# Attention, cumulative-max attention and expert choice on one core: where two candidate lists are merged, and how the last sample is searched

## The chip, the cores and the metric

The kernel runs on one core of a Trainium2 chip. The metric is the device time of one execution in microseconds; lower is better. A core has five engines that run their own instruction streams: PE (TensorE, matmuls and transposes), DVE (VectorE), ACT (ScalarE), POOL (GpSimd) and SP (SyncE, which here only issues DMAs). Streams are tied together by semaphores.

## The reference

The input is four samples of 128 channels by 64x64 positions, so 4 x 4096 tokens of 128 numbers. Three steps follow one another, each with a residual:

```python
x = x + conv_attn(group_norm(x))      # three 1x1 convs, 4096x4096 softmax attention
t = tokens(x)
t = t + cummax_attn(layer_norm(t))    # 8 heads: exp(s - cummax(s)), cumsum, v weighted, mean of heads
t = t + expert_choice(layer_norm(t))
```

The change lies in the last step. It is an expert choice: the experts choose the tokens.

```python
logits = einsum('bsd,ed->bse', x, gate_w) + gate_b      # 64 experts
probs = softmax(logits, axis=1)                          # over the 4096 tokens of a sample
vals, idx = top_k(probs.transpose(0, 2, 1), 8)           # 8 tokens for each expert
pooled = einsum('bked,bke->bed', x[idx], vals)           # weighted sum of those 8 tokens
h = gelu([pooled, 1] @ weight1[e])                       # 129 x 512, own weights for each expert
out = [h, 1] @ weight2[e]                                # 513 x 128
outputs.at[idx].add(out * vals)                          # scattered back to the 8 tokens
```

For every sample and expert the kernel needs the eight largest logits, their rows, the sum of the exponentials of all 4096 logits, and the eight rows of x weighted and summed. The weights of the 64 experts are 512 KB each.

## The kernel before, in words

The first layer takes the span to about 1450 us and is not touched. Then `loop` (L2150) goes over 32 blocks of 512 tokens: four samples of eight blocks. It is software-pipelined: in one turn PE does the keys (`f_pk`) of the block six ahead, and for the block itself the values (`f_pv`, 64 matmuls in each of four parts), the totals (`f_pt`), the products (`f_po` L1174, L1186), and the carried sums (`f_ltr`, `f_str`, `f_etr`, `f_mc`). The turn ends when DVE adds the result into `t` (L1192). The order on every engine is the order of the program: PE, ACT, DVE and POOL are written out by hand, as is the order of DMAs on SP.

The gate (norm, logits, choice) runs beside this, some blocks behind. `make_plan` (L2091) puts each of its steps into a slot of a block: `at(i, slot, fn, ...)` notes it, and `run(m, slot)` emits it. The slots of a turn are 1, 2, "D", 3, 4, "T" and "G" in that order. The steps of the gate are:

- `gate_stats`, `gate_root`, `gate_close`: mean and root of the variance of each token.
- `gate_norm` (ACT L1272, or DVE L1267): the normalised rows `f_x`, stored by SP to a table in DRAM, `f_table`.
- `gate_turn` (L1281): four transposes `f_gtr` and a copy to SBUF (L1285).
- `gate_logits` (L1287): `f_pl`, then DVE writes the logits `f_lg` (L1295) and takes the eight largest of this block (MAX8, L1299). A partition holds one expert; the two halves of 64 partitions hold two halves of a block's tokens.
- `merge_half` (L1311): the eight largest over the blocks of a sample, for each half. `candidate_rows` (L1326): `max_index` over all logits of the sample (2048 a partition, `f_ci`).
- `merge_halves` (L1336): `both_halves` brings the two halves together with eight small matmuls `f_pw` (L1320), then some fourteen small DVE operations make the final eight values and their row numbers `f_at`.
- `gathers` (L1370): four indirect DMAs on POOL fetch rows from the table. `exps` (L1377): exponentials of all logits. `count`, `denominators`, `select` (L1397), `pool` (L1440, `f_pp`): weights and the pooled rows.

All of `f_pl`, `f_pw`, `f_mc`, `f_etr`, `f_pq`, `f_pp` and `f_htr` share one PSUM buffer with the tag "sm".

The last sample can't wait for a later block. Its first seven blocks are merged in slot "T" of block 31, and `last_choice` (L1474) does the rest after the loop: the norm and logits of block 31, a merge of its eight best with those found before, the exponentials, and pooling (`f_pp`, `f_ce`, `f_pc`). Between these stand `fill`s (L1460): transposes `f_etb` of `t` that are wanted later, put back by `put_back` (L1465). Then `experts` (L1625) takes 16 groups of four experts: `f_ph`, gelu, `turn` (`f_htr`), `f_eo`, and one or two `turn_back`s (`f_otr`). `late_choice` (L1556) does what is left of the last sample's counting on DVE beside the first groups. Twenty-one experts have rooms that can be filled from block 26 on (`load_into`, `load_rooms` L2224); the other 43 are loaded in halves when `f_ph` and `f_eo` have freed a room (L1597, L1604). `stores` writes the output.

Of the kernel before, what the change touches and what calls it, by code (L numbers as in the profile page):

```python
# [17 lines left out]
def conv_attn_hybrid_kernel(  # L18
# [809 lines left out]
    def fast():  # L828
# [365 lines left out]
        def gate_setup(rest):  # L1194
# [28 lines left out]
            for j in range(16):  # L1223
                nc.gpsimd.memset(spare(3, 48 + j, 1), float(j))
# [35 lines left out]
        def gate_norm(m, split=False):  # L1260
            b, k = blocks[m]
            x2_of[m] = x2 = env.xl_pool(f"f_x2_{m}")
            for c in range(CPB):
                src = t[:, b * NCH + k * CPB + c, :]
                rs, nb = env.grs[:, ring(m), c : c + 1], env.gnb[:, ring(m), c : c + 1]
                if split and c % 2:
                    nc.vector.tensor_scalar(  # L1267
                        out=x2[:, c, :], in0=src, scalar1=rs, scalar2=nb,
                        op0=ALU.mult, op1=ALU.add,
                    )  # L1270
                else:
                    nc.scalar.activation(x2[:, c, :], src, AF.Identity, bias=nb, scale=rs)  # L1272
            if not split:
                rows_ = table[b].rearrange("(h k c p) d -> h k p c d", h=2, k=deep[b], p=P)
                for h in range(2):
                    nc.sync.dma_start(out=rows_[h, k], in_=x2[:, 2 * h : 2 * h + 2, :])
# [10 lines left out]
        def gate_logits(m):  # L1287
# [11 lines left out]
            nc.vector.max(out=sel[b]["cand"][:, bass.ts(k, 8)], in_=env.lg[b][:, k, :])  # L1299

        ex_at = lambda i: env.e2b[:, bass.ts(i, BLK)]
        g_at = lambda k: env.e1b[:, 5 * BLK + k * C : 5 * BLK + (k + 1) * C]
# [8 lines left out]
        def merge_half(b, count):  # L1311
            st = sel[b]
            st["both"] = both = small_tile(b, "both", 16, bufs=1)
            nc.vector.max(out=both[:, 0:8], in_=st["cand"][:, : count * 8])
# [11 lines left out]
        def candidate_rows(b, count):  # L1326
            st = sel[b]
            both = st["both"]
            ci = small_tile(b, "ci", 8, dtype=U32, bufs=1)
            nc.vector.max_index(out=ci, in_max=both[:, 0:8], in_values=flat_lg(b, 0, count))  # L1330
            nc.vector.tensor_scalar(
                out=both[:, 8:16], in0=ci, scalar1=env.base[:, b : b + 1], scalar2=None,
                op0=ALU.add,
            )

        def merge_halves(b):  # L1336
            st = sel[b]
            pw = both_halves(st["both"], f"f_pw_{b}").rearrange("p s (v k) -> p v s k", v=2)
            found = spare(3, 0, 32).rearrange("p (v s k) -> p v s k", v=2, s=2)
            nc.vector.tensor_copy(found, pw)  # L1340
            first8 = spare(3, 32, 16).rearrange("p (v k) -> p v k", v=2)
            st["top"] = top = first8[:, 0]
            vals, rows16 = spare(3, 0, 16), spare(3, 16, 16)
# [7 lines left out]
            for h in range(2):  # L1351
                half = slice(h * E, (h + 1) * E)
                nc.vector.tensor_copy(own[half], first8[half, :, 4 * h : 4 * h + 4])
            st["src"] = src = small_tile(b, "src", 5, bufs=1)
            nc.vector.tensor_copy(src[:, 0:4], own[:, 0])
            nc.vector.tensor_copy(src[:, 4:5], top[:, 7:8])
            hit = spare(2, 0, 64).rearrange("p (k j) -> p k j", k=4)
            nc.vector.tensor_tensor(
                hit, own[:, 1].unsqueeze(2).to_broadcast([P, 4, 16]),
                spare(3, 48, 16).unsqueeze(1).to_broadcast([P, 4, 16]), ALU.is_equal,  # L1360
            )
            nc.vector.tensor_tensor(
                hit, hit, rows16.unsqueeze(1).to_broadcast([P, 4, 16]), ALU.mult,
            )
            rowf = small_tile(b, "rowf", 4, bufs=1)
            nc.vector.tensor_reduce(rowf, hit, AX.X, ALU.add)
            st["at"] = at = small_tile(b, "at", 4, dtype=I32, bufs=1)
            nc.vector.tensor_copy(at, rowf)

        def gathers(b, lo, hi):  # L1370
            for k in range(lo, hi):
                nc.gpsimd.indirect_dma_start(
                    out=g_at(k), out_offset=None, in_=table[b],
# [3 lines left out]
        def exps(b, j):  # L1377
            st = sel[b]
            if j == 0:
                st["ce"] = ce = small_tile(b, "ce", 5, bufs=1)  # L1380
                st["sums"] = small_tile(b, "sums", 4, bufs=1)
                nc.scalar.activation(ce, st["src"], AF.Exp, bias=st["neg"])
# [57 lines left out]
        def pool(b):  # L1440
            dd = sel[b]["dd"]
            pp = sm(f"f_pp_{b}", E)
            for k in range(4):
                nc.tensor.matmul(pp, g_at(k), dd[:, k, :], start=(k == 0), stop=(k == 3))
# [28 lines left out]

        def last_choice():  # L1474
# [5 lines left out]
            for n, tag in enumerate(("kv", "kv", "kv", "kv", "t", "o", "kv", "kv")):  # L1480
                fill(n, tag, n % 2)
            put_back(0, act, 2)
            gate_root(m, 1)
            gate_close(m, 1)
            gate_norm(m, split=True)
            put_back(2, act, 2)
            gate_turn(m, dve)
            fill(8, "kv")
            gate_logits(m)
            put_back(6, act, 2)  # L1490
            fill(9, "kv", 1)
            late = st["cand"][:, bass.ts(k, 8)]
            pw = both_halves(late, "f_pw1")
            fill(10, "kv")
            fill(11, "kv", 1)
            merged = small_tile(b, "merged", 24, bufs=1)
            nc.vector.tensor_copy(merged[:, 0:8], top0)
            nc.vector.tensor_copy(merged[:, 8:24], pw.rearrange("p s k -> p (s k)"))
# [7 lines left out]
            st["ce"] = ce = small_tile(b, "ce", 5, bufs=1)  # L1506
            nc.scalar.activation(ce, src, AF.Exp, bias=neg)
            nc.scalar.activation(chd, lg, AF.Exp, bias=neg)
            st["sums"] = sums = small_tile(b, "sums", 4, bufs=1)
            nc.scalar.activation(  # L1510
                flat_lg(b, 0, NBLK), flat_lg(b, 0, NBLK), AF.Exp, bias=neg,
                accum_out=sums[:, 0:1],
            )
            put_back(4, act)
            put_back(10, act, 2)
# [4 lines left out]
                out=chd, in0=chd, scalar=ce[:, 4:5], in1=chd, op0=ALU.is_ge, op1=ALU.mult  # L1520
            )
            pp = sm("f_pp3", E)
            for kk in range(4):
                nc.tensor.matmul(pp, g_at(kk), dd[:, kk, :], start=(kk == 0), stop=False)
            pc = ps.tile([P, BLK], F32, tag="x", name="f_pc")
            for j in range(2):
                nc.tensor.transpose(pc[:, bass.ts(j, P)], chd[:, bass.ts(j, P)], ident)
            ct = ex_at(1)[:, HB:].rearrange("p (j x) -> p j x", j=2)
            nc.vector.tensor_copy(ct, pc[:, : 2 * P].rearrange("p (j x) -> p j x", j=2))
            x2 = x2_of[NB - 1]  # L1530
            for h in range(2):
# [5 lines left out]
                if h == 0:  # L1537
                    pq = ps.tile([P, BLK], F32, tag="x", name="f_pq3")
                    nc.tensor.matmul(pq[:, 0:1], env.pair, sums[:, 0:1], start=True, stop=True)
            nc.vector.reciprocal(env.den[:, b : b + 1], pq[:, 0:1])  # L1540
            dr = env.e1b[:, 7 * BLK + 2 * C : 7 * BLK + 2 * C + E]
            nc.vector.tensor_scalar(
                out=dr, in0=env.pair[:, :E], scalar1=env.den[:, b : b + 1], scalar2=0.5,
                op0=ALU.mult, op1=ALU.mult,
            )
            pr = ps.tile([P, BLK], F32, tag="t", name="f_pr3")
            nc.tensor.matmul(
                pr[:, :E], ones.to_broadcast([P, P]), dr, start=True, stop=True
            )
# [6 lines left out]
        def late_choice(g):  # L1556
            if g < 2:
                count(B - 1, g, g + 1)
            elif g == 2:
                select(B - 1)  # L1560

        def late_count():
            b = B - 1
            pq = sm("f_pqb", 2)
            nc.tensor.matmul(pq, env.pair, sel[b]["sums"][:, 2:4], start=True, stop=True)
# [59 lines left out]
        def experts():  # L1625
# [9 lines left out]
            hold = [  # L1635
                env.rest.tile([P, FC, QG, QW], F32, tag="xl", name=f"f_hs_{i}", bufs=3)
                for i in range(2)
            ]
            for tile_ in hold:
                nc.gpsimd.memset(tile_, 0.0)  # L1640
# [79 lines left out]
            n = 12  # L1720
            for g in range(EG):
                turn(g)
                late_choice(g)
                for _ in range(2 if g < NB - 12 - EG else 1):
# [366 lines left out]
        def make_plan():  # L2091
# [14 lines left out]
            at(NB - 1, 1, gate_root, NB - 2, 1)  # L2106
            at(NB - 1, 1, gate_close, NB - 2, 1)
# [4 lines left out]
            for m in range(NB - 10, NB - 2):  # L2112
                i = NB - 5 + (m - NB + 10) // 2
                at(i, "D" if m == NB - 6 else "G", gate_norm, m)
                at(i + 1, 1 + m % 2, gate_turn, m)
                at(i + 1, (2 if i == NB - 2 else 3) + m % 2, gate_logits, m)
            at(NB - 1, 2, gate_norm, NB - 2)
            at(NB - 1, 3, gate_turn, NB - 2)
            at(NB - 1, 4, gate_logits, NB - 2)
            for b in range(B - 2):  # L2120
# [3 lines left out]
                at(i, 3, merge_halves, b)  # L2124
                at(i, 4, exps, b, 0)
                for k in range(4):
                    at(i + k, "G", gathers, b, k, k + 1)
# [13 lines left out]
            at(NB - 2, "G", select, last)  # L2141
            at(NB - 1, 1, denominators, last)
            at(NB - 1, 4, pool, last)
            at(NB - 1, 4, merge_half, B - 1, NBLK - 1)
            at(NB - 1, 4, candidate_rows, B - 1, NBLK - 1)
            at(NB - 1, "T", merge_halves, B - 1)
            at(NB - 1, "T", gathers, B - 1, 0, 4)
            at(NB - 1, "T", root_table)

        def loop():  # L2150
            make_plan()
            normals(LAG + 1)
            for n in range(LAG, NB + LAG):
# [13 lines left out]
                value(m, 0)  # L2167
                value(m, 1)
                slot(2)
                if n < NB:  # L2170
# [27 lines left out]
                totals(2)  # L2198
                totals(3)
# [16 lines left out]
                if n == NB + 2:  # L2216
                    load_into(slot_of(env.e1a, 2))
                if n == NB + LAG - 2:
                    load_into(slot_of(env.e1a, 3))
# [4 lines left out]
        def load_rooms():  # L2224
            for room in (slot_of(env.ama, 0), slot_of(env.ama, 1), slot_of(env.ama, 2),
                         slot_of(env.ama, 3), env.wvs,
                         env.held[:, bass.ts(3, HD)]):
                load_into(room)
            for i in range(CPB):
                load_into(slot_of(env.amb, i))  # L2230
            load_into(slot_of(env.e2a, 0))
            load_into(slot_of(env.e2a, 1))
# [93 lines left out]
```

## Time and profile before

| what | value |
|---|---|
| time, median of 3 runs (lowest, highest) | 2317.12 us (2316.6, 2318.71) |
| profiled execution, its own time | 2323.74 us |
| its span, first to last instruction | 2322.0 us |
| mean granted TensorE clock | 0.992 |
| PE, DVE, ACT, POOL busy | 97%, 62%, 47%, 8% of the span |
| block, from one addition to `t` to the next | 20.9 to 22.4 us in most blocks |
| block 14 and block 22 | 27.4 and 29.8 us |
| first `f_ph` of the experts | 2222.69 us |
| last expert weight landed | 2289.9 us |

The page's durations are those of one execution, which took 6.6 us longer than the median of the runs. In a row of the timeline or of the costliest groups the letters after the line number say what was written from what ("f_pw<-f_both,ident"), and the bracket at the end gives the idle time of that engine just before, and what ended it. "PEclk" is the clock that was granted, as a share of the full one.

### The profile page before, as it was taken

The page shows a single profiled execution, that of the slowest core. Times are in us where ns is not written, and L with a number is a line of the kernel's source. Part 1 is how long each engine was busy: PE and PEld are TensorE (multiplying, and loading weights), DVE is VectorE, ACT ScalarE, POOL GpSimd, SP SyncE. Part 2 cuts the span into 40 slices and gives each one's busy share as a digit, 9 for nine tenths or more (in the row PEclk, how much of TensorE's full clock was granted, in tenths as well). Part 3 has the DMA queues.
Part 4 walks back from the last instruction along what each step waited for, and adds up shares of the span by engine and source line. Part 5 has one row for each costly group of instructions (what it writes and reads, how often), then busy time and mean ns, then how long its engine had stood idle before and what let it go on. Part 6 is the DMA issues. An engine that isn't in the chain of part 4 may idle for free.

```text
span 2322.0 us, 43150 instructions
## 1 busy us (share of the span) xinstructions
PE 2247.8 (97%) x18352; PEld 1168.5 (50%) x18352; DVE 1444.6 (62%) x2361; ACT 1086.4 (47%) x1324; POOL 175.9 (8%) x364
## 2 busy tenths in 40 slices
PE   7999999999999999999999999999999999999997
PEld 3544444444444444444444444456565556556663
DVE  7666565655665565565556656568777677865623
ACT  2343333433333443334455444455666566566641
POOL 0000000000000000000000000012211222122311
PEclk9999999999999999999999999999999999999989
DMA  2000010000010000000000000011122121114578
GB/s 77 32 12 17 9 45 8 17 8 9 17 45 9 9 17 9 9 25 27 9 5 5 10 5 5 20 44 41 41 58 53 43 59 46 52 47 129 153 279 303
DMA packets 78555, 104.77 MB, mean 45 GB/s; under 512 B 8976, under 2 KB 44816, under 8 KB 78352
## 3 DMA queue, kind: packets, MB, share of 16 engines
q1 hardware_dynamic: 77264, 99.81, 14.0%
q8 instruction: 146, 2.39, 0.4%
q0 software_dynamic: 512, 1.05, 0.2%
q10 hardware_dynamic: 576, 1.05, 0.1%
q14 instruction: 57, 0.47, 0.1%
HBM read 78.55 MB, written 17.04 MB: 41 GB/s over the span
## 4 chain that ended last, share of the span: by engine, by line
PE 86%; DVE 6%; ACT 3%; DMA 3%; issue 1%; SPq 0%; POOL 0%; another core or an unknown queue 0%; ACTq 0%; DVEq 0%; POOLq 0%
PE av L1939 36%; PE sc L1914 18%; PE f_pv L1128 9%; PE f_pk L973 8%; PE f_pt L1151 3%; PE f_po L1174 2%; PE pd L1965 1%; DMA x<-in_x_dram 1%; ACT f_e1a L980 1%; PE pa L1887 1%; PE pe L1861 1%; PE f_po L1186 1%; DVE f_e1a L981 1%; DVE f_e1a L982 1%; PE f_pl L1291 1%
## 5 line engine op out<-in xcount | busy, mean ns | idle before, releaser
L1939 PE MATMUL av<-pr,am 64*128 64x512 f32 x4096 | 978.0, 592 | 2.9 <-ACT pr L1919 2.9
L1919 ACT ACTIVATE pr<-sc 128x1024 f32<-128x1024 f32 x512 | 523.6, 1023 | 782.7 <-PE sc L1914 769.8
L1926 DVE TENSOR_TENSOR acc<-acc,pr 128x1024 f32<-128x1024 f32 x480 | 586.6, 1222 | 485.4 <-ACT pr L1919 481.1
L1939 PEld LDWEIGHTS av<-pr,am 64*128 64x128 f32 x4096 | 401.6, 187 | 472.9 <-issue 457.9
L1914 PE MATMUL sc<-e,e 64*128 64x512 f32 x2048 | 534.4, 591 | 4.7 <-DMA e<-side 4.7
L1914 PEld LDWEIGHTS sc<-e,e 64*128 64x128 f32 x2048 | 201.6, 187 | 236.6 <-issue 229.0
L1128 PE MATMUL f_pv<-f_held,f_ama 128*32 128x256 f32 x4096 | 242.7, 387 | 5.5 <-ACT f_e1a L980 4.5
L973 PE MATMUL f_pk<-f_held,f_ama 128*128 128x512 f32 x512 | 234.9, 603 | 0.0
L1133 ACT ACTIVATE f_amb<-f_pv 128x1024 f32<-128x1024 f32 x128 | 130.8, 1023 | 141.7 <-PE f_pv L1128 140.9
L981 DVE TENSOR_TENSOR f_e1a<-f_e1a,f_held 128x1024 f32<-128x1024 f32 x128 | 157.5, 1231 | 46.6 <-ACT f_e1a L980 46.2
L980 ACT ACTIVATE f_e1a<-f_pk 128x1024 f32<-128x1024 f32 x128 | 129.9, 1025 | 117.8 <-PE f_pk L973 57.8
L1128 PEld LDWEIGHTS f_pv<-f_held,f_ama 128*32 128x32 f32 x4096 | 131.3, 111 | 102.2 <-issue 15.1
L982 DVE TENSOR_REDUCE f_e1a<-f_e1a 128x8 f32<-128x1024 f32 x128 | 155.3, 1218 | 3.5
L973 PEld LDWEIGHTS f_pk<-f_held,f_ama 128*128 128x128 f32 x512 | 92.5, 190 | 109.1 <-issue 101.4
L1092 POOL COPY f_held<-f_e1a 32x32 f32<-32x32 f32 x128 | 30.5, 238 | 924.1 <-DVE f_e1a L1074 563.3
L1151 PE MATMUL f_pt<-f_amb,f_held 128*32 128x128 f32 x1920 | 83.0, 276 | 0.8 <-ACT f_amb L1133 0.8
L918 POOL MEMSET f_held<- 128x1024 f32 x1 | 1.0, 956 | 1036.3 <-DVE xn L1852 1036.3
L1151 PEld LDWEIGHTS f_pt<-f_amb,f_held 128*32 128x32 f32 x1920 | 59.9, 109 | 10.3 <-issue 5.2
L1192 DVE TENSOR_TENSOR t<-t,f_po 128x512 f32<-128x512 f32 (+1 forms) x33 | 22.1, 671 | 55.6 <-PE f_po L1186 55.6
L956 ACT ACTIVATE f_xl<-t,ln_nb,ln_rs 128x128 f32<-128x128 f32 x128 | 52.8, 490 | 0.8 <-PE pa L1887 0.8
L1272 ACT ACTIVATE f_x<-t,f_gnb,f_grs 128x128 f32<-128x128 f32 x126 | 51.3, 482 | 0.4 <-DVE f_gnb L1253 0.4
L1923 DVE COPY acc<-pr 128x1024 f32<-128x1024 f32 x32 | 22.2, 694 | 39.3 <-ACT pr L1919 39.3
(287 smaller groups left out, 1776.6 us busy)
## 6 DMA issues: line engine op xcount, KB each, us to landing
f_e2a<-f_rd SPq DMA_DIRECT2D x128, 128.0 KB, 2.9
xr<-in_xtok_dram SPq DMA_DIRECT2D x32, 256.0 KB, 3.0
f_table<-f_x SPq DMA_DIRECT2D x62, 128.0 KB, 1.8
out_dram<-t SPq DMA_DIRECT2D x14, 512.0 KB, 3.8
x<-in_x_dram SPq DMA_DIRECT2D x12, 512.0 KB, 7.0
e<-e SPq DMA_DIRECT2D x32, 128.0 KB, 2.2
f_ama<-f_rd SPq DMA_DIRECT2D x16, 256.0 KB, 3.8
f_e1b<-f_rd SPq DMA_DIRECT2D x16, 256.0 KB, 6.0
```

What stands on the lines that cost most here:

```text
L956: nc.scalar.activation(xl[:, c, :], t[:, b * NCH + i, :], AF.Identity, bias=ln_nb[:, b, i : i + 1], scale=ln_rs[:, b, i : i + 1],)
L973: nc.tensor.matmul(pk[:, i, :], xt_at(n)[:, bass.ts(c, P)], env.wks[:, bass.ts(i, BLK)], start=True, stop=True,)
L980: nc.scalar.activation(flat, pk.rearrange("p i x -> p (i x)"), AF.Silu)
L981: nc.vector.tensor_mul(ks, ks, env.qb)
L982: nc.vector.tensor_reduce(s[:, (n % GB) * CPB + c, :], ks, AX.X, ALU.add)
L1128: nc.tensor.matmul(pv[a * CH : (a + 1) * CH, i, :], xt_at(m)[:, bass.ts(c * NA + i, CH)], env.wvs[:, bass.ts(a, HH * C)], start=True, stop ...
L1133: nc.scalar.activation(env.amb[:, bass.ts(c, HD)], pv.rearrange("p i x -> p (i x)"), AF.Silu)
L1151: nc.tensor.matmul(env.pt[i * CH : (i + 1) * CH, :], lhs, rhs, start=i not in env.begun, stop=False, skip_group_check=True,)
L1914: nc.tensor.matmul(sc[:, u, :], e2[halves[u], p, :], e1[halves[u], cols], start=True, stop=True,)
L1919: nc.scalar.activation(pr, sc, AF.Exp)
L1926: nc.vector.tensor_add(acc, acc, pr)
L1939: nc.tensor.matmul(av, am[h, j, :], pr[h, u, :], start=(j == 0), stop=(j == NCH - 1))
```

## The change

1. For samples 0 and 1 `merge_halves`, the first part of `exps` and the four gathers move one block later; `candidate_rows` stays. The gathered rows go to one of two places by the sample's number, and `places`, the numbers that are compared with, has a tile of its own (32 columns).
2. The last sample is searched in two parts: blocks 24 to 29 in slots "W" and 3 of block 31 (`max_index` over 1536), block 30 alone by `new_best` (over 256). The merge is then 32 wide instead of 16 and stands in a new slot "O", before the last totals.
3. The exponentials of blocks 24 to 30 are taken in slot "O" relative to the maximum known then (`old_exps`); after block 31 a factor `ce[5]`, the exponential of old minus new maximum, corrects sum and weights, and `bar` is the eighth value on the old scale. Only the 256 columns of block 31 are left for after the loop. The denominator goes through the bank of `f_pc`.
4. The last sample's four gathers are spaced: one in slot "O", one after two fills, one after the norm, one after the copy of `f_gtr`. Two memsets of 128x512 on POOL (L1640) move from the start of `experts` to slot 4 of block 31.
5. The gate steps of blocks 28 to 31 are placed anew, with new slots "V" and "W"; `denominators` of sample 2 moves to slot "T" of block 30, its `pool` into `last_choice`, its `select` beside group 4 of the experts. There are ten fills instead of twelve, so groups 4 and 5 have a second `turn_back`.
6. Three rooms are loaded earlier (one after block 28, two after block 30), and the order in `load_rooms` is different. There are as many rooms as before.
7. `late_choice` counts in four parts of 512 or fewer columns at group 0, with more at groups 1 to 4.

The diff, cut:

```diff
@@ merge_halves, gathers
-    hit = spare(2, 0, 64).rearrange("p (k j) -> p k j", k=4)
+    hit = room[:, 4 * w : 12 * w].rearrange("p (k j) -> p k j", k=4)
...
-g_at = lambda k: env.e1b[:, 5 * BLK + k * C : 5 * BLK + (k + 1) * C]
+g_at = lambda b, k: env.e1b[:, (5 + b % 2) * BLK + k * C : (5 + b % 2) * BLK + (k + 1) * C]
@@ the last sample
+def old_exps():
+    b = B - 1
+    st = sel[b]
+    st["neg0"] = st["neg"]
+    st["sums"] = small_tile(b, "sums", 5, bufs=1)
+    nc.scalar.activation(
+        flat_lg(b, 0, NBLK - 1), flat_lg(b, 0, NBLK - 1), AF.Exp, bias=st["neg0"],
+        accum_out=st["sums"][:, 0:1],
+    )
+
+def new_best():
+    b = B - 1
+    best = sel[b]["both"][:, 8:16]
+    find_rows(b, 8, NBLK - 2, NBLK - 1)
+
+def last_rooms():
...
+    for tile_ in env.hold:
+        nc.gpsimd.memset(tile_, 0.0)
@@ last_choice
-for n, tag in enumerate(("kv", "kv", "kv", "kv", "t", "o", "kv", "kv")):
+fill(0, "kv")
+fill(1, "kv", 1)
+row_numbers(b, 1, 2)
+gathers(b, 1, 2)
+pool(B - 2)
+for n, tag in ((2, "kv"), (3, "kv"), (4, "t"), (5, "o")):
     fill(n, tag, n % 2)
-put_back(0, act, 2)
 gate_root(m, 1)
 gate_close(m, 1)
-gate_norm(m, split=True)
+gate_norm(m, (1, 3))
+row_numbers(b, 2, 3)
+gathers(b, 2, 3)
+put_back(0, act, 2)
+gate_turn(m, dve)
+row_numbers(b, 3, 4)
+gathers(b, 3, 4)
 put_back(2, act, 2)
-gate_turn(m, dve)
-fill(8, "kv")
+fill(6, "kv")
 gate_logits(m)
...
-nc.scalar.activation(chd, lg, AF.Exp, bias=neg)
-st["sums"] = sums = small_tile(b, "sums", 4, bufs=1)
-nc.scalar.activation(
-    flat_lg(b, 0, NBLK), flat_lg(b, 0, NBLK), AF.Exp, bias=neg,
-    accum_out=sums[:, 0:1],
-)
+nc.scalar.activation(chd, lg, AF.Exp, bias=neg, accum_out=sums[:, 1:2])
+st["bar"] = bar = small_tile(b, "bar", 1, bufs=1)
+nc.scalar.activation(bar, top[:, 7:8], AF.Exp, bias=st["neg0"])
@@ late_choice
-if g < 2:
-    count(B - 1, g, g + 1)
-elif g == 2:
-    select(B - 1)
+if g == 0:
+    for i in range(4):
+        tally(2 * i, min(2 * i + 2, NBLK - 1), st["bar"], 1 + i)
+elif g == 1:
+    nc.vector.tensor_reduce(st["sums"][:, 0:1], st["sums"][:, 1:5], AX.X, ALU.add)
+    tally(NBLK - 1, NBLK, st["ce"][:, 4:5], 1)
+elif g == 2:
+    nc.vector.scalar_tensor_tensor(
+        out=old, in0=old, scalar=st["bar"], in1=old, op0=ALU.is_ge, op1=ALU.mult
+    )
+elif g == 3:
+    nc.vector.tensor_scalar_mul(old, old, st["ce"][:, 5:6])
+elif g == 4:
+    select(B - 2)
@@ make_plan
-at(NB - 1, 1, gate_root, NB - 2, 1)
-at(NB - 1, 1, gate_close, NB - 2, 1)
...
+end = NB - 1
+at(end, 1, gate_turn, NB - 4)
+at(end, 1, gate_root, NB - 2, 1)
+at(end, 1, gate_close, NB - 2, 1)
+at(end, 1, gate_norm, NB - 2, range(CPB))
+at(end, "V", gate_turn, NB - 3)
+at(end, 2, gate_logits, NB - 4)
+at(end, "W", gate_turn, NB - 2)
+at(end, "W", gate_logits, NB - 3)
+at(end, "W", merge_half, B - 1, NBLK - 2)
+at(end, 3, candidate_rows, B - 1, NBLK - 2)
+at(end, 3, gate_logits, NB - 2)
+at(end, 3, new_best)
+at(end, 4, last_rooms)
+at(end, "O", merge_halves, B - 1, 1)
+at(end, "O", gathers, B - 1, 0, 1)
+at(end, "O", old_exps)
+at(end, "O", root_table)
 for b in range(B - 2):
     i = (b + 1) * NBLK + 6
     at(i - 1, 3, merge_half, b, NBLK)
     at(i, 2, candidate_rows, b, NBLK)
-    at(i, 3, merge_halves, b)
-    at(i, 4, exps, b, 0)
+    at(i + 1, 2, merge_halves, b)
+    at(i + 1, 4, exps, b, 0)
     for k in range(4):
-        at(i + k, "G", gathers, b, k, k + 1)
+        at(i + 1 + k, "G", gathers, b, k, k + 1)
...
-at(NB - 2, "G", select, last)
-at(NB - 1, 1, denominators, last)
-at(NB - 1, 4, pool, last)
-at(NB - 1, 4, merge_half, B - 1, NBLK - 1)
-at(NB - 1, 4, candidate_rows, B - 1, NBLK - 1)
-at(NB - 1, "T", merge_halves, B - 1)
-at(NB - 1, "T", gathers, B - 1, 0, 4)
-at(NB - 1, "T", root_table)
+at(NB - 2, "T", denominators, last)
@@ loop, load_rooms
 value(m, 0)
+run(m, "V")
 value(m, 1)
 slot(2)
+run(m, "W")
...
 totals(2)
+run(m, "O")
 totals(3)
...
 if n == NB + 2:
     load_into(slot_of(env.e1a, 2))
+    load_into(slot_of(env.ama, 2))
 if n == NB + LAG - 2:
-    load_into(slot_of(env.e1a, 3))
+    for room in (slot_of(env.e1a, 3), slot_of(env.ama, 0), slot_of(env.e2a, 0)):
+        load_into(room)
```

## The prediction

> **What bounds the kernel now.** I read the busy shares on the page first, then the waits of TensorE (PE) after 1250 us, then windows over the places where those waits lie, then the chain of waits.
>
> ```profile
> PE 2247.8 (97%) x18352; PEld 1168.5 (50%) x18352; DVE 1444.6 (62%) x2361; ACT 1086.4 (47%) x1324; POOL 175.9 (8%) x364
> ```
>
> PE is the bound nearly everywhere: only what it waits for, or what slows its clock, can be won before the experts. The waits (total us, times, longest):
>
> ```profile
> PE f_pw L1320 <- DVE f_lg L1295: 7.2, 2, 3.6
> PE f_pw L1320 <- DVE f_both L1331: 3.5, 2, 2.6
> ```
>
> The first row is the merging of halves for samples 0 and 1, at 1846 and 2027 us, in blocks 14 and 22. The timeline of PE has one of them, and the windows (length, then PE, PEld, DVE, ACT, POOL busy, PE clock, DMA share, GB/s) show what comes after:
>
> ```profile
> 2027.36 0.61 PE L1320 MATMUL f_pw<-f_both,ident 128*64 128x16 f32 x8 [3.62 <-DVE f_lg L1295]
> ...
> 1846.00:1852.00 6.00, 5.96 (x76) 3.28 (x76) 2.58 (x15) 1.35 (x2) 0.00 (x0) 0.72 0.01 3
> 2027.40:2034.30 6.90, 6.90 (x72) 3.36 (x72) 2.52 (x15) 1.02 (x1) 0.00 (x0) 0.55 0.01 2
> 2205.00:2210.00 5.00, 4.43 (x37) 3.78 (x36) 3.06 (x15) 3.08 (x5) 3.35 (x4) 1.00 0.98 364
> 2210.00:2214.40 4.40, 2.12 (x21) 1.27 (x20) 1.67 (x4) 2.29 (x2) 1.45 (x3) 1.00 0.36 128
> 2214.40:2222.70 8.30, 6.97 (x33) 6.04 (x33) 2.96 (x12) 5.58 (x8) 0.00 (x0) 0.51 0.22 63
> 2222.70:2227.20 4.50, 4.50 (x21) 1.58 (x22) 0.00 (x0) 1.32 (x3) 0.00 (x0) 0.50 0.32 103
> 2256.00:2290.00 34.00, 30.02 (x354) 17.17 (x356) 3.15 (x13) 9.34 (x22) 1.06 (x7) 1.00 0.98 357
> ```
>
> After each wait the clock is down: 64 f_pv take 5.00 and 6.49 us where they take 3.66 elsewhere. In the tail it is at half from 2214.4 to 2227.2. Between 2210 and 2227 the DMA engines are two thirds idle; from 2227 they are full, until the last expert weight lands at 2289.9. The chain of waits passes through both:
>
> ```profile
> 2208.64 2.83 another core or an unknown queue
> 2211.49 0.70 DVE f_e1b L1285
> ...
> 2222.69 3.64 PE f_ph L1665 x16
> ...
> 2284.10 5.78 DMA f_e2b<-in_fw_dram
> ```
>
> The timeline of POOL says what the unnamed 2.83 us is, for DVE starts when POOL ends:
>
> ```profile
> 2209.50 0.94 POOL L1372 DMA_INDIRECT f_e1b<-f_table,f_at  x1 [0.30 <-issue]
> 2210.45 1.00 POOL L1640 MEMSET f_hs<- 128x512 f32 x2
> ```
>
> So the end of the kernel hangs on when the first f_ph frees a room for the first reload (issued 2224.6), and from there on a weight stream of fixed length.
>
> **What the Trainium skill says.** "TensorE: Matmul & The Clock Gate", section "Part 1: The HAM clock gate (the "warmup" mystery)": after an idle window of about 3.4 us the array's clock is halved, and takes about one busy window to return. The trace agrees: idle 3.62, then clock 0.55 for 6.9 us. It also halves after 2.6 us of idling at block 29, so I take no sharp threshold. "SBUF — State Buffer", section "Who interferes with whom": DVE and GpSimd share a port pair, held for whole instructions. The trace agrees in part: a gather takes 3.09 us beside DVE's select and 0.94 alone. The 2.83 us above ends with POOL, but the page exempts copies out of PSUM, so its cause stays open. Same page, section "A bandwidth-pool intuition that's wrong (but worth ruling out)": some 358 GB/s between HBM and a core; the last window above has 357. "ScalarE activation tables: per-element evaluation and per-set limits", section "What a function is on this engine": a table load is 1283 ns; here 1.28 us.
>
> **The change part by part.**
>
> *Halves of samples 0 and 1 merged a block later.* Removed: the stall, since DVE has a whole block in which to finish max_index (2.27 us) and the four key operations (1.2 each) before f_pw is due. By blocks (time from one addition to t to the next): block 14 took 27.4 against 21.83 for its place in the row of blocks; minus 0.41 for f_pw, which only moves, 5.15 go. Block 22 took 29.79; minus 21.83, minus 1.05 for pool(0), minus 0.4, 6.5 go. Sum 11.65. Added: the merge chain of some 14 small DVE operations (1846.7 to 1849.1, 2.4 us) now stands ahead of that block's keys and its f_lg. f_etr in slot 4 uses the one "sm" bank of PSUM, which f_lg frees. In block 15 f_lg ended at 1872.98, with the chain 1875.05 at most; f_etr is due at about 1874.5, so it waits 0.55. Twice, 1.1. The exponentials (4.2 us with two table loads) move one block on with what they collided with: PE waited 0.3 there before and will again, nothing. The two sets of gathers move too, onto a POOL that is 8% busy; g_at has two places now, so nothing waits for the pool of the sample before. The 16 more memsets come early, behind PE work. **Loop: −10.6, from −9 to −11.7.**
>
> *Last sample, block 31.* PE's waits there (0.94 for the denominators, 0.59 for pool, 0.96 for f_pw) lie in moved work and go: −2.5. pool(2), 1.1 us of PE, moves behind the last f_po, where PE idled: −1.1. Against it the merge, 32 wide, is now in slot "O", ahead of the last products: on DVE the copy of the totals (L1168) stands behind it until about 2201.8, and f_po L1186 waits some 1.25 for that. That leaves −2.35. Going through the queues one by one with the durations of the timeline, I get the end of the last f_po at 2202.9 (2204.84 before), −1.9, and take this. What waits for L1168 is PE, then t, then everything after.
>
> *After block 31.* Statistics and x2 keep their durations: f_gtr ends near 2207.6. Its copy started at 2211.49, 2.1 after f_gtr, behind four gathers of 0.95 spaced 1.25 and the memsets. Only one gather (0.95) can now stand in front of it, the memsets being in block 31. It ends at 2207.8 to 2209.0 where it ended at 2212.2. Then, with the old durations: f_pl 2208.9, f_pw1 2210.6, ce 2211.9. The late exponential is 256 wide instead of 2048 and the bar is a single column: ACT has some 1.5 us less to do ahead of put_back, which is not on the path. pp3 at 2213.0 needs the last gather, issued at about 2209.0 and landed 3.5 later at the median (2212.5): just in time, at most (7.1) 3 late. f_pc, with the denominators, 2214.0. f_ph at 2216.85 against 2222.69: −5.85. Idle of PE in these six us is some 2.6, in four pieces of at most 1.05, so I expect the clock to stay up; then f_ph x16 takes half its 3.64, and the first reload goes out 6.7 earlier. The room loads move forward on SP (one at block 28, two at block 30), past stores of normalised rows that land in 1.8 us and are gathered a block or more later; they cost nothing there, and the hole before the reloads stays open, about 8 us instead of 15.
>
> I take off 1.2 for a gather that holds DVE up beside L1168 or L1288, or lands late. **Tail: −5.5, from 0 to −9.**
>
> *Experts.* The counting of the last sample (2.6 us of DVE at g=0, then reduce, 1792-wide operations) and select(2) (2.32) are on DVE, which is busy 3.15 in the 34 us of the window 2256 to 2290; PE has some 5.2 us between the first turn and the second. Hidden: nothing. Two fills fewer and two turn_backs more (0.44 each) fall under the stream: 43 experts of 512 KB, 22.5 MB in 2224.6 to 2289.9, 65 us at the DMA limit, then 32 us of adding back and storing. If that cover is gone PE's 30.0 of 34 us is next.
>
> **Sum.** −10.6 − 5.5 = −16.1. The profiled execution took 2323.7 (span 2322.0 and 1.7 around it), 6.6 over the median of the runs, 2317.1. 2307.6 for a profile, 2301.0 for the median.
>
> **The rivals.** (A) As above, 2301, own range 2298 to 2304: **0.60**. (B) The clock halves in the tail after all. The idle pieces add to 2.6 in 6 us, and before, 1.72 and 0.56 close together were enough. The work from pp3 on stays at its old durations, f_ph comes at 2219.3, and the tail gives 3: 2303.5, **0.17**. (C) The transfer hides it: experts start early but the room loads still fill the queues to 2210, and the stream ends when it did. Against it: the hole is 15 us, longer than the shift. Loop alone, 2306.5: **0.12**. (D) The wait comes back elsewhere: in blocks 15 and 23 f_etr waits 2 to 4 us each, with a slower clock after, eating most of the loop's gain; 2309 to 2317: **0.06**, of which 0.03 within 0.2% of before. (E) Slower: the same place with a longer delay. The chain, the exponentials' table loads and the new gathers (locked against DVE, 3.1 instead of 0.95) put f_lg 5 us late at f_etr; 64 f_pv at half clock add up to 2.8, so each block loses 7 to 8 where it gained 5 to 6.5: loop +4. The same lateness in block 31 (L1168) sends PE into the tail at half speed, some 11 us of work on which 2.5 more are lost: 2323. It decides from a lateness of about 4 to 5 us; I work out 0.55. For it: f_etr has one bank; against it: no view shows POOL beside the chain. **0.05**.
>
> **How the numbers follow.** A measurement can tell about 0.2% (4.6 us) from no change. A, B, C and half of D are faster: 0.92; same 0.03; slower 0.05. The likeliest gives 2301.0. Loop −11.7 and tail −9 give 2296.4, a little under it is possible where I took nothing; C with the loop at −9 gives 2308. 2295.5 to 2308.5 leaves out D and E and the edge of B and C.
>
> **What would show it.** Right: no f_pw wait on f_lg of 3.6; blocks 14, 15, 22 and 23 at 21.5 to 22.5 (23 for the one with pool) and their clock at 1.0; f_etr waiting under 1; POOL's gathers apart, the copy of f_gtr within 1.2 of f_gtr's end; the clock over 0.9 between f_pw1 and f_ph; a DMA hole of about 8 us and a full stream of 65 behind it. Wrong: blocks 15 or 23 above 24, a clock of 0.5 in the tail (B), first reload early but last weight no earlier beyond the loop's gain (C), an f_po wait over 2 in block 31, or a new PE wait for DVE between the turns of groups 0 and 1.

## The result, and the profile after

The changed kernel takes 2306.1 us in the median (2303.7 to 2310.7, 6 runs) against 2319.1 us for the kernel before beside it (2316.6 to 2322.9, 6 runs). The ratio is 0.9938, 95% interval 0.9926 to 0.9951: of 2319.1 us that is 14.4 us less, from 11.4 to 17.2. The two medians differ by 13.0. The forecast was 16.1 less.

The two profiles differ by more, 20.2 us: the changed kernel's profiled execution took 2303.66 us and was its fastest run, the one of before 2323.74, above all six of its runs. The page of the changed kernel, its span and its first line:

```profile
span 2301.8 us, 43187 instructions
PE 2238.5 (97%) x18352; PEld 1163.8 (51%) x18352; DVE 1447.1 (63%) x2380; ACT 1092.2 (47%) x1328; POOL 174.4 (8%) x380
```

PE is busy 9.3 us less with as many instructions. That is mostly clock, whose mean rose from 0.992 to 0.995. The rest is waiting. The waits of PE after 1250 us, changed kernel (total, times, longest):

```profile
PE f_pw L1325 <- DVE f_both L1338: 2.6, 1, 2.6
...
PE f_po L1186 <- issue: 1.1, 1, 1.1
...
PE f_etr L1064 <- DVE f_lg L1298: 0.7, 2, 0.3
```

The two f_pw waits of 3.6 us on f_lg are gone. The timeline of PE has the f_pw of sample 0, now in block 15, without a wait:

```profile
1856.69 0.41 PE L1325 MATMUL f_pw<-f_both,ident 128*64 128x16 f32 x8
```

One f_pw wait, of sample 2, is left as it was. The f_po wait in block 31 and the two f_etr waits are new, and both were in the forecast.

The windows over the end of the changed kernel (stretch, length, PE, PEld, DVE, ACT, POOL busy, clock, DMA share, GB/s):

```profile
2195.00:2199.00 4.00, 3.21 (x28) 2.19 (x28) 2.11 (x11) 2.64 (x4) 0.96 (x2) 1.00 0.56 203
2199.00:2203.50 4.50, 3.10 (x22) 2.86 (x22) 2.21 (x9) 3.22 (x7) 0.00 (x0) 0.87 0.37 107
2203.50:2207.10 3.60, 3.54 (x16) 0.60 (x16) 0.00 (x1) 0.59 (x1) 0.00 (x0) 0.50 0.19 60
...
2240.00:2270.00 30.00, 26.77 (x349) 15.99 (x351) 2.70 (x11) 8.45 (x20) 0.91 (x6) 1.00 0.96 350
```

The hole in the transfers is there, some 8 us with one load in it; the stream after it is as full as before. The clock falls later than before, but it is at half again when f_ph starts. The chain of waits of the changed kernel has that f_ph, and nothing unnamed ahead of it:

```profile
2193.13 0.88 ACT f_x L1275 x2
...
2203.56 3.64 PE f_ph L1735 x16
...
2258.26 5.92 DMA f_held<-in_fw_dram
```

From the additions to t in the DVE timeline (L1192) the profiles of all runs can be laid beside one another block by block. Blocks 1 to 25 repeat to 0.02 us from one execution to the next, but for 14 and 22 where they hold the stall, so they can be trusted singly; blocks 26 to 29 and the tail can't.

| stretch, us | before | changed | difference |
|---|---|---|---|
| to the first addition (layer 0) | 1548.79 | 1547.42 | −1.37 |
| block 14 | 27.40 | 21.83 | −5.57 |
| blocks 15 and 16 | 43.26 | 44.37 | +1.11 |
| block 22 | 29.79 | 22.74 | −7.05 |
| blocks 23 and 24 | 43.26 | 44.37 | +1.11 |
| blocks 26 to 29 | 65.22 | 63.68 | −1.54 |
| blocks 30 and 31 | 36.02 | 34.43 | −1.59 |
| last addition to the end of the span | 117.09 | 111.80 | −5.29 |

### The profile page after: what moved, and what is told of

It is laid out like the page before. It is cut to its first block, busy times and chain, and to the rows that moved or that the text cites. A ratio compares the mean times of both kernels' runs of the same rounds, so it can differ in the third digit from the quotient of the medians.

```text
span 2301.8 us, 43187 instructions
## 1 busy us (share of the span) xinstructions
PE 2238.5 (97%) x18352; PEld 1163.8 (51%) x18352; DVE 1447.1 (63%) x2380; ACT 1092.2 (47%) x1328; POOL 174.4 (8%) x380
## 3 DMA queue, kind: packets, MB, share of 16 engines
q1 hardware_dynamic: 77264, 99.81, 13.9%
## 4 chain that ended last, share of the span: by engine, by line
PE 87%; DVE 6%; ACT 3%; DMA 2%; issue 1%; SPq 0%; POOL 0%; ACTq 0%; DVEq 0%; POOLq 0%
PE av L2009 37%; PE sc L1984 18%; PE f_pv L1128 9%; PE f_pk L973 8%; PE f_pt L1151 3%; PE f_po L1174 2%; PE pd L2035 1%; PE f_po L1186 1%; ACT f_e1a L980 1%; PE pa L1957 1%; DMA x<-in_x_dram 1%; PE pe L1931 1%; DVE f_e1a L981 1%; DVE f_e1a L982 1%; PE f_pl L1294 1%
## 5 line engine op out<-in xcount | busy, mean ns | idle before, releaser
L1128 PE MATMUL f_pv<-f_held,f_ama 128*32 128x256 f32 x4096 | 237.5, 381 | 6.1 <-ACT f_e1a L980 5.1
L1128 PEld LDWEIGHTS f_pv<-f_held,f_ama 128*32 128x32 f32 x4096 | 129.2, 110 | 100.7 <-ACT f_e1a L980 11.9
L1151 PEld LDWEIGHTS f_pt<-f_amb,f_held 128*32 128x32 f32 x1920 | 60.0, 109 | 10.4 <-issue 5.2
L1192 DVE TENSOR_TENSOR t<-t,f_po 128x512 f32<-128x512 f32 (+1 forms) x33 | 22.1, 671 | 56.0 <-PE f_po L1186 56.0
```

Source lines behind the costliest of these rows:

```text
L1128: nc.tensor.matmul(pv[a * CH : (a + 1) * CH, i, :], xt_at(m)[:, bass.ts(c * NA + i, CH)], env.wvs[:, bass.ts(a, HH * C)], start=True, stop ...
L1151: nc.tensor.matmul(env.pt[i * CH : (i + 1) * CH, :], lhs, rhs, start=i not in env.begun, stop=False, skip_group_check=True,)
```

## The experiments

Of e3, e4, e5 and e9 there is one execution each. Only their profiles are read, since one total (2316.7, 2322.7, 2308.6 and 2307.1 us) says little where six runs of one kernel lie up to 7 us apart.

**One part alone, and all but one.**

e1 is the kernel before with:

```diff
-at(i, 3, merge_halves, b)
-at(i, 4, exps, b, 0)
+at(i + 1, 2, merge_halves, b)
+at(i + 1, 4, exps, b, 0)
...
-at(i + k, "G", gathers, b, k, k + 1)
+at(i + 1 + k, "G", gathers, b, k, k + 1)
```

> The kernel before, with only the merge of halves, the first exponentials and the gathers of samples 0 and 1 one block later. Theory (the parts add): blocks 14 and 22 fall to 21.8 and 22.7 us, blocks 15, 16, 23 and 24 get 0.75 and 0.36 us longer, in all -10.4 us of the span; the tail stays as it was, the first f_ph 17.8 us after the last addition to t and the stream of weights 65 us long. Ratio to before about 0.9955. Rival (the gain needs the other parts, since the later exponentials and gathers collide with steps that the full change moved away): blocks 15 to 17 take 1 to 3 us more than that, and the gain is 5 to 8 us.

2311.5 us, ratio 0.9964 (0.9954 to 0.9974). Blocks 14 to 16 took 21.83, 23.14 and 21.23 us, blocks 22 to 24 took 22.73, 23.13 and 21.24: as in the full change, to 0.01. From block 13 to 25 it is −10.4, and the rival falls. The ratio says 8.4 us (6.0 to 10.7). What didn't fit was the tail: the first f_ph came 13.97 us after the last addition, not 17.8. Of these 3.8 us, 2.0 are the copy of f_gtr, which came 4.53 us after the addition and not 6.58. The other 1.8 go with the clock, which in the five us ahead of f_ph was 1.00 and not 0.50.

> The changed kernel, with the merge of halves, the first exponentials and the gathers of samples 0 and 1 back in their old block. Theory (the parts add): blocks 14 and 22 are back at 27.4 and 29.8 us, +10.4 us on the changed kernel; what is left of the gain is the last sample's, 4 to 8 us against before (ratio 0.9965 to 0.998). Rival (the transfer hides the earlier tail, so all of the gain was the loop's): no more than 1 us faster than before, ratio 0.9995 to 1.0005.

(The same lines the other way in the changed kernel.) 2316.6 us, ratio 0.999 (0.9981 to 0.9999). Blocks 14 and 22 took 27.53 and 28.34 us. In block 22 PE waited 3.61 us for f_pw as before, but the 64 f_pv after it took 5.04 us, not 6.49: what the clock takes after the same wait varies. What is left is 2.3 us, between 0.2 and 4.4: less than expected for the last sample. It is more than nothing, but the interval reaches into the rival's range, up to 1 us. With e1's 8.4 it makes 10.7 of the 14.4; the intervals are too wide to call that a gap. From the last addition to the end it took 112.0 us, as in the changed kernel.

**Stall or clock.**

```diff
 def merge_halves(b):
     st = sel[b]
+    if b < 2:
+        idle = ps.tile([P, BLK], F32, tag="x", name=f"f_idle_{b}")
+        for _ in range(30):
+            nc.tensor.transpose(idle[:, :P], ident, ident)
```

> The kernel before, with 30 transposes of the identity (about 3.4 us of work for PE, read by nobody) in front of each f_pw of samples 0 and 1, where PE stands still. The wait stays, only PE is no longer idle in it. Theory (the stall is one cost, the halved clock after it another): f_pw comes no earlier, but the 64 f_pv after it take 3.66 us in both blocks; block 14 falls by 1.3 us and block 22 by 2.8. Rival (the slower f_pv come from something else, as the merge chain on DVE or its traffic): f_pv stay at 5.0 and 6.5 us and nothing is gained.

The timeline of PE in block 22 of this kernel:

```profile
2021.43 3.49 PE L1341 MATMUL f_idle<-ident 128*128 128x128 f32 x30
2025.11 0.41 PE L1320 MATMUL f_pw<-f_both,ident 128*64 128x16 f32 x8 [0.18 <-DVE f_lg L1295]
2025.45 3.66 PE L1128 MATMUL f_pv<-f_held,f_ama 128*32 128x256 f32 x64
```

f_pw comes no earlier, and f_pv take 3.66 us where they took 6.49. Block 14 fell by 1.54 and block 22 by 3.04. So of the 12.6 us that left blocks 14 and 22 from the profile of before to that of the changed kernel, 4.6 were the clock, 7.2 the stall and 0.8 the two f_pw, which only moved.

**What held the copy of f_gtr.**

e4 is the kernel before with the two memsets (L1640) in `last_rooms`, as in the change:

```diff
+at(NB - 1, 4, last_rooms)
```

> The kernel before, with the two memsets of 128x512 on POOL moved from the start of the experts to slot 4 of block 31; the four gathers stay back to back. Theory (the copy of f_gtr is held up by POOL's memsets alone): the copy starts as soon as f_gtr is done, 2 us earlier against the last addition to t, as in the changed kernel beside a gather. Rival 1 (gathers hold it too): it starts when the last gather ends, 1 us earlier than before. Rival 2 (POOL has nothing to do with it): the copy starts 6.6 us after the addition to t, as before. The first f_ph moves by as much.

The copy came 4.58 us after the last addition. But this proves nothing for the theory, since it came at 4.53 in e1 and e3 as well, with the memsets where they were. The row of DVE in before, then the rows of e1 in the timelines of DVE and POOL:

```profile
2211.49 0.69 DVE L1285 COPY f_e1b<-f_gtr 128x512 f32<-128x512 f32 x1 [2.85 <-remote]
...
2200.16 0.69 DVE L1285 COPY f_e1b<-f_gtr 128x512 f32<-128x512 f32 x1 [0.81 <-PE f_gtr L1284]
```

```profile
2200.22 0.94 POOL L1372 DMA_INDIRECT f_e1b<-f_table,f_at  x1 [0.31 <-PE f_gtr L1284]
2201.16 1.00 POOL L1640 MEMSET f_hs<- 128x512 f32 x2
```

The copy of e1 starts 0.06 us ahead of the fourth gather. In the profile of before f_gtr, gather and memsets stand at the same distances, and the copy starts only when POOL is done. If POOL is the cause, two microseconds hang on 0.06. Only one of the three executions with that order (before, e1, e3) lost them. Whether the copy itself can be held was the question of the next one:

```diff
-for tile_ in env.hold:
-    nc.gpsimd.memset(tile_, 0.0)
...
+for tile_ in env.hold * 2:
+    nc.gpsimd.memset(tile_, 0.0)
 row_numbers(b, 2, 3)
 gathers(b, 2, 3)
```

> The changed kernel, with the two memsets of 128x512 on POOL taken out of block 31, doubled (four of 0.5 us) and put in front of the third gather of the last sample, so that they run when the copy of f_gtr (DVE, out of PSUM) comes due. The copy waits on no semaphore but PE's. In the profile of before it started 2.0 us late, when gather and memsets ended, but in three other runs with the same order it slipped in 0.06 us ahead of the gather. Theory (POOL and DVE exclude each other, and whoever comes second waits until POOL has a gap): the copy starts when the last memset ends, 1 to 1.3 us later against the last addition to t than in the changed kernel (5.5 to 5.9 instead of 4.54), and the first f_ph as much later. Rival (the late start in before was something else): the copy starts at 4.5, only the two gathers after the memsets are late.

The copy started at 6.26, but not for the reason given. DVE's timeline in e5, then POOL's:

```profile
2195.41 2.56 DVE L1270 TENSOR_SCALAR f_x<-t,f_grs,f_gnb 128x128 f32<-128x128 f32 x2
...
2198.54 0.69 DVE L1288 COPY f_e1b<-f_gtr 128x512 f32<-128x512 f32 x1 [0.52 <-PE f_gtr L1287]
```

```profile
2195.88 1.93 POOL L1529 MEMSET f_hs<- 128x512 f32 x4
```

The two operations that write f_x took 2.56 us instead of 0.60, and end 0.16 after the last memset; the copy waited for PE, and PE for them. So in this execution the memsets on POOL held a DVE operation from SBUF to SBUF for their whole length, and it is not idle time of DVE that shows it but a duration. For the copy out of PSUM in before, POOL as the cause stays inferred from one execution. The clock fell too (0.52 in the five us ahead of f_ph), and f_ph came 16.39 after the addition (13.56 in the changed kernel).

**The clock in the tail.**

```diff
+pc = ps.tile([P, BLK], F32, tag="x", name="f_pc")
+for _ in range(7):
+    nc.tensor.transpose(pc[:, 3 * P :], ident, ident)
 pp = sm("f_pp3", E)
...
+for _ in range(4):
+    nc.tensor.transpose(pc[:, 3 * P :], ident, ident)
```

> The changed kernel with 11 transposes of the identity, read by nobody: 7 in front of the first f_pp of the last sample, where PE idles 0.81 us, and 4 behind f_pc, where it idles 0.52. Theory (PE's clock fell because it idled 1.3 us of 3.5 here): the clock is 1.0 in the 5 us ahead of f_ph and in f_ph, the 16 f_ph take 1.9 instead of 3.6 us, and the first reload comes 1 us earlier after the last addition to t (14.5 instead of 15.5). Rival (the clock falls for another reason, as the wait ahead of f_ph itself): f_ph stay at 3.6 us, the first reload at 15.5 or later.

Ratio 0.9949 (0.9933 to 0.9966). The windows over the 5 us ahead of f_ph and over f_ph, of e6 and then of e9 (below), which has no such transposes:

```profile
2205.26:2210.26 5.00, 4.08 (x34) 3.49 (x32) 2.42 (x9) 3.52 (x8) 0.00 (x0) 1.00 0.34 105
2210.26:2213.86 3.60, 3.60 (x32) 1.87 (x36) 0.91 (x4) 2.10 (x3) 0.00 (x0) 1.00 0.42 122
...
2200.87:2205.87 5.00, 3.31 (x29) 2.89 (x27) 2.63 (x11) 3.75 (x8) 0.00 (x0) 1.00 0.29 79
2205.87:2209.47 3.60, 3.60 (x32) 1.86 (x36) 0.91 (x4) 2.10 (x3) 0.00 (x0) 1.00 0.47 160
```

In e6 the clock stayed up, and the first reload came 14.77 us after the last addition instead of 15.50. But e9, whose work on PE up to f_ph is that of the changed kernel, kept its clock too, and its reload came at 14.28; e7 is like it. With PE busy 3.3 of the 5 us each time, the clock ahead of f_ph was 0.88 in the changed kernel, 0.98 in e8 and e11, and 1.00 in e7 and e9. So one execution can't show that the transposes kept it up. From the reload to the end e6 took 98.1 us (96.3 in the changed kernel), and no time was won. Over all profiles this last stretch varies from 94.8 to 98.9 us, so 0.7 is lost in it.

**Merge in T, rooms, select.**

e7 is the changed kernel with the four steps of slot "O" in "T", of which the first:

```diff
-at(end, "O", merge_halves, B - 1, 1)
+at(end, "T", merge_halves, B - 1, 1)
```

> The changed kernel with the merge of the last sample's halves, its first gather, the exponentials of blocks 24 to 30 and the table load in slot T of block 31, behind the totals' last copy, instead of in slot O ahead of it. Theory (the copy L1168 stands behind the merge chain and makes f_po L1186 wait 1.1 us): that wait is gone, block 31 takes 17.2 instead of 18.3 us, and the first f_ph comes 1.1 us earlier. Rival (the chain only moves: it now delays the addition to t or the statistics, and the gather comes late for f_pp): block 31 falls, but the time from the last addition to t to f_ph grows from 13.6 us by as much.

Ratio 0.9943 (0.9924 to 0.9962). Block 31 took 17.00 us, the f_po wait was gone, and f_ph came 13.34 after the addition: the theory, to 0.2. In a total that varies by several us it is not seen.

> The changed kernel with the rooms loaded at the times and in the order of the kernel before. Theory (the hole of 8 us in the transfers between the last room and the first reload covers it): the room loads end about 4 us later, 3 to 4 us of hole are left, the first reload and the end stay: ratio to before as the changed kernel's, 0.992 to 0.995, and the time from first reload to the end 96 us. Rival (the early loads are what the earlier reload needed, the queues are still full when it comes): the weights land 3 to 4 us later, from first reload to the end 99 us or more.

(The loads of ama[0], ama[2] and e2a[0] back in load_rooms, in its old order.) Ratio 0.9953 (0.9935 to 0.9971), just above what was expected, with an interval that overlaps the changed kernel's (0.9926 to 0.9951). The first reload came 15.15 after the addition, and the end 95.2 after that, not later than elsewhere. But the edit hardly moves the loads. Room loads on SP, in us ahead of the last addition to t:

| | before | changed | e8 |
|---|---|---|---|
| one into f_ama | 40.1 | 38.5 | 38.9 |
| next one into f_ama | 17.6 | 15.1 | 15.5 |
| first of two into f_e2a | 17.0 | 15.7 | 14.9 |

Block 31 is 2 us longer in before. So these loads go out at nearly the same places in all three kernels, whatever the program's order, and in e8 the room transfers end about 1 us later than in the changed kernel, not 4. By these rows point 6 of the change has next to no effect, and what late rooms would cost was not tested.

> The changed kernel with the select of sample 2 (2.32 us on DVE, 2048 columns) back in slot G of block 30, where it was, instead of beside group 4 of the experts. Theory (DVE has no room for it at the start of block 31, where the last sample's logits and search stand in a row): PE waits 0.5 to 1.5 us more in block 31 for f_pl, f_pw or f_po, and block 31 takes 18.5 to 19.5 us instead of 18.0 to 18.3. Rival (it was hidden where it was): block 31 stays within 0.2 of 18.0 to 18.3. In neither does the time from the first f_ph to the end change by more than 1 us.

Block 31 took 19.75 us, a little over what was expected. Its waits of PE in e9, in that block:

```profile
PE f_pl L1294 <- DVE f_lg L1298: 1.2, 1, 1.2
PE f_po L1186 <- issue: 1.1, 1, 1.1
```

The first of them is the select's, and isn't there in the changed kernel. Its move is worth 1.5 us in block 31, which no total shows. From the first f_ph to the end e9 took 99.3 us, the changed kernel 98.2 and e11 99.2.

**What is left to win, and the change once more.**

e10 is e7 and:

```diff
-at(NB - 3, 2, merge_halves, last)
+at(NB - 3, "D", merge_halves, last)
...
-if m:
+if m and m != NB - 4:
     weigh_rows(m)
...
 slot(3)
+if m == NB - 4:
+    weigh_rows(m)
```

> The changed kernel with three moves. The merge of the last sample is in slot T of block 31, as in the run before. The merge of sample 2 in block 29 moves from slot 2 to slot D, behind work of PE that needs no DVE. In block 28 the weighing of rows (L1122), which waits for a transfer, stands behind slot 3 on DVE instead of slot 1, so that the first f_lg doesn't wait behind it. Theory (waits of PE of 2.6 us in block 29 and 0.2 to 1.5 in block 28, and the slow clock after them, are what is left to win): no f_pw wait of 2.6 us, block 29 at 15.2 us and block 28 at 16.1 to 16.5 in every run, clock 1.0 in both; 4 to 7 us faster than the changed kernel, ratio to before 0.991 to 0.992. Rival (the merge chain in front of the totals' copy makes f_po wait in block 29 instead, and the weighed rows come late for f_po in block 28): block 29 at 17 or more, 28 as long as before, and 1 to 2 us at most are won, the move to T.

> The changed kernel unaltered, beside the others on one chip. Theory (its profile was one of its fastest executions, and the kernel before's one of its slowest): 12 to 16 us faster than before in the median, ratio 0.993 to 0.995, while a profile may show a block 28 of 17 to 21 us and a block 29 of 17.8 to 20.7. Rival (the 20 us between the two profiles are the true gain): ratio 0.991 to 0.992.

e11: 2307.2 us, ratio 0.9941 (0.9927 to 0.9955), so the 20 us between the first profiles are not the gain. e10: 2301.5 us, ratio 0.9918 (0.9904 to 0.9931), faster than both kernels, by 5.3 us than the changed one in the ratios; its slowest run (2304.0) is below the fastest of e11 (2304.8). How the three moves share this was not measured. Its blocks 28 and 29, by windows:

```profile
2120.30:2136.92 16.62, 16.04 (x317) 11.28 (x317) 7.44 (x27) 11.11 (x17) 4.25 (x9) 1.00 0.73 178
2136.92:2152.98 16.06, 15.29 (x315) 10.38 (x315) 12.26 (x33) 10.51 (x17) 3.55 (x5) 1.00 0.41 113
```

No f_pw wait is left in the loop. Block 28 is 0.1 above what was expected, and block 29 isn't at 15.2: 0.6 us of a new wait (f_pl on the first copy of the merge chain, L1352) takes the place of 2.6.

## Why the prediction was right

**Loop, −10.6.** Measured −10.4, and e1 has it alone. The 11.65 of stall and slow clock went as worked out. The f_etr waits were put at 0.55 each and were 0.35 each. That blocks 16 and 24 get 0.36 longer was put at nothing ("PE waited 0.3 there before and will again"): the f_pv wait of 0.30 on ACT in block 15 stayed although the exponentials left, and block 16, where they went, got one of 0.29. Blocks 15 and 23, at 23.1, missed the 21.5 to 22.5 of the list of signs: they took 22.4 before, and f_pw and the f_etr wait came on top.

**Block 31, −1.9.** The f_po wait behind the merge chain was put at 1.25 and was 1.10. Over the eight profiles with one or the other of the two orders (before, e1, e3, e4; changed, e2, e5, e8) blocks 30 and 31 together took 36.0 us each time and 34.2 to 34.4: −1.6 to −1.8. Block 31 alone lost 2.0 to 2.3, but block 30 got 0.45 longer, with 0.45 more work on PE for the denominators that moved there. e9 bears out the place of select.

**After block 31, −3.6 of the tail's −5.5.** This term was too large: the step "Its copy started at 2211.49 … Only one gather (0.95) can now stand in front of it" took a hold-up for a fixture that showed in one execution of three. Without the hold-up, from the last addition to the end the order of before took 114.7, 114.2 and 113.8 us (e1, e3, e4), and the changed order 111.8, 112.0, 112.8, 110.4 and 112.4 (changed, e2, e6, e8, e11). In the mean that is 114.2 and 111.9, −2.3. With −10.4 and −1.7 the sum is −14.4. That the ratio says the same to a tenth is luck, with an interval of 11.4 to 17.2. The new path up to f_ph was worked out well: some 13.9 us after the last f_po, and 13.56 measured after the addition. What it was set against was unusually slow: 17.78 in before, where e1, e3 and e4 took 13.97, 15.79 and 15.33. Not settled is how the 2.3 are shared between the spaced gathers, the short exponential, the two turn_backs and a clock that differs between executions.

**The clock stays up.** In both profiles of the changed kernel it did not: f_ph took 3.64 us as before in the first, and in e11 its clock was 0.55. This was in part rival B. What decides it is not known: the forecast's measure, idle pieces and the longest of them, is the same in e7 and e9, where the clock stayed at 1.00. B's price of 2.5 us was high for this kernel: the first reload came 14.28 us after the addition in e9, and 15.15 to 16.10 in four profiles with a lower clock (e8, e11, changed, e2), 0.9 to 1.8 later. With the merge in T it was 2.4 (14.42 in e7, 16.85 in e10). The end of the span doesn't follow this within its scatter.

**Experts, rooms, stream.** From the first f_ph to the end it took 98.4 to 100.7 us in the order of before (before, e1, e3, e4) and 97.2 to 99.2 in the changed one (changed, e2, e8, e11), so the work beside the experts is hidden, as said. The rooms weren't tested (e8). A correction to the description ahead of the prediction: the order of the DMAs on SP isn't written out by hand. Only PE, ACT, DVE and POOL are; SP's order follows from the program by the scheduler, which fits that the loads stayed where they were. The 357 GB/s in the last of the prediction's windows include its idle end. From 2256 to 2284 the kernel before moves 381, so the stream isn't bound at the 358 that stand beside them.

**The level.** 2301.0 was forecast and 2306.1 measured, within the 2295.5 to 2308.5 that were stated, but outside A's own 2298 to 2304 and, by the number alone, next to the 2306.5 of rival C. Of these 5 us, 2.0 are the kernel before, whose median was 2317.1 in the first three runs and 2319.1 in six. The three terms above make 1.7, and 1.4 is what the medians differ less than the ratio says. As a difference 14.4 lies between A's 16.1 and C's 10.6, and nearer to A.

## What to carry to other kernels

Take a stall apart into waiting and slow clock, and price both: here 7.2 us in which PE stood still cost 4.6 more afterwards in one profile, and the second part differs between executions. Before a gap in one profile is priced as something that a change removes, ask whether it hangs on a race of some hundredths of a microsecond, and see whether it comes back in a second execution. In this kernel a chain of small operations on DVE is better placed behind the copy that PE waits for than ahead of it (e7: block 31 took 17.0 us for 18.0 to 18.3). A merge behind work of PE that needs no DVE was one of the three moves of e10.

## What the runs showed of the hardware

The clock's answer to the same idle time differs between executions. Block 29 has the same f_pw wait of 2.56 us in all profiles but e10's. Windows over it, before and then changed:

```profile
2149.71:2168.89 19.18, 16.62 (x315) 10.93 (x315) 12.36 (x34) 10.23 (x15) 5.22 (x10) 0.91 0.32 91
```

```profile
2137.79:2155.57 17.78, 15.22 (x315) 10.36 (x315) 12.35 (x33) 10.23 (x15) 5.22 (x10) 1.00 0.33 96
```

With the same instructions PE is busy 1.4 us longer in the first. In eleven of the twelve profiles with that wait the clock of the block fell to between 0.84 and 0.91; only the changed kernel's first was spared. In e7 the clock was 0.84 there and the block took 20.74. "TensorE: Matmul & The Clock Gate", section "Part 1: The HAM clock gate (the "warmup" mystery)", of the Trainium skill has the clock fall after at least one idle window of about 3.4 us, and says that the window runs freely. A wait of 2.56 us is shorter, and the clock fell all the same, so here the measurement decides. That the same wait ends differently would fit a window that runs freely, but no run here shows the windows themselves.

Much of the scatter of this kernel sits there and in block 28, which took from 16.8 to 21.5 us in the profiles without e10's moves. DVE waits 4.8 to 6.1 us for a transfer (f_e2a from f_rd), f_lg waits behind it, PE for f_lg up to 1.5 us in f_pl, and the clock then falls in some executions: to 0.91 in e1, e4 and e6 and 0.84 in e8.

Two DVE operations from SBUF to SBUF beside memsets on POOL took four times their length (2.56 us in e5, 0.60 in the changed kernel). This agrees with "SBUF — State Buffer", section "Who interferes with whom", of the skill: DVE and GpSimd share a pair of ports, the instruction that gets it first keeps it to its end, and the other stands still; tensor_scalar is among the operations that can need it. The ports themselves no run shows. The copy of f_gtr, which reads PSUM, showed no such stretch beside a gather: 0.69 us in the changed kernel.
